# Where the last heads of layer 1 are stored, and when their output product runs

## The chip, the cores and the metric

The kernel runs on one core of a Trainium2 chip. Its five engines work at the same time and are tied together by semaphores: TensorE (PE in the profile, with its weight loads as PEld), VectorE (DVE), ScalarE (ACT), GpSimd (POOL), and SyncE (SP), which here issues the DMA transfers. The metric is the device time of one execution, in microseconds; lower is better. Times are given as the median of several runs.

## The reference

Four attention layers are applied one after the other to `x`, of shape 4 batches x 1024 rows x 256 features, with 16 heads of 16 features each and a context of 77 rows per batch. All arithmetic is in 32-bit floats.

- Layer 0: layer norm, causal self-attention over the 1024 rows and the 77 context rows, then two norms and a feed-forward block of width 1024.
- Layer 1: two attentions side by side. A linear one over the context (`lin`) and a sliding-window one over the last 64 rows (`win`):

```
linear_out = (linear_out / (normalizer + EPS_DEN)).reshape(B, T_dec, D_MODEL)
window_out = jnp.einsum('bhts,bshd->bthd', probs, v_win).reshape(B, T_dec, D_MODEL)
combined = jnp.concatenate([linear_out, window_out], axis=-1)
return residual + combined @ Wout
```

- Layer 2: cross-attention to the context. The scores are multiplied by a given weight per entry and masked, then softmax, values, output product, residual and layer norm.
- Layer 3: cross-attention to the context with heads of 64 features, RMS norm before it, residual after it.

The change concerns the end of layer 1 (`combined @ Wout` for the last half of the heads of the last batch) and the start of layer 2.

## The kernel before, in words

`x` stays on the chip for the whole kernel, one tile per batch (`xs[b]`, 8 row blocks of 128 rows x 256 features). A manual schedule is in force (L94): each engine executes its instructions in the order in which the Python code emits them.

*Memory.* `wpool` holds weights; each of its tags is one slot that successive weights share. Tag `s1`, 2048 floats per partition, first holds layer 0's query and key weights and from unit (3,3) of layer 0 on layer 1's (`w1q`, L1010, made by `plain_pair`, L116). `work` holds the working tiles of layers 0 and 1; the tag `lw` in it has four slots of 1024 floats per partition. After layer 1 `work` is closed (`first.close()`, L1663), and the pool `late`, with the working tiles of layers 2 and 3, takes its place in memory (L1664), so that a tile of `late` can only be written when the tiles of `work` have had their last readers. `small` lives through the kernel; its tag `sT` has two slots. In PSUM, `sm` has three slots in rotation for all small products and transposes, `big` two for scores, and `pv` one.

*Layer 1.* A unit is a batch and a `quad` of four heads; there are 16 units, and the loop at L1650 to L1654 runs each unit's maxima beside the exponentials and products of the unit before. `weights1` (L1179) makes the tiles `lin` and `win` for each pair of quads, that is for half of the heads, and returns the six items that fill them. An item's result goes through `settle` (L533): ACT copies the product from PSUM, PE transposes it, DVE divides and writes it to `lin` or `win` (L551).

`combine1(b, half)` (L1246) adds the output product of one half to `x`. It is a generator of 12 steps: for each of four pairs of row blocks, four PE transposes of `lin` and `win` into `ptc` (L1254), an ACT copy to `cT` (L1256) and a step end; another step end; four products of two matmuls' depth each, eight matmul records in the profile, into `po1` (shown as `po`), a DVE addition to `x` (L1267) and a step end. For all halves but the last it runs as a job beside the units (L1609 to L1613). The last one, `combine1(3, 1)`, runs alone at L1662, after everything pending has been flushed (L1661) and before `work` is closed.

*Jobs.* A `Job` (L436) has a generator, its number of steps `n`, and a start and an end share `a` and `b`: at share s of the stage it has done n x (s - a) / (b - a) steps, rounded up. With `rest` true what is left is done at the end of the stage.

*Start of layer 2.* In this order (L1664 to L1669): `late` is opened, SP loads the keys `kb`, the first weight and mask tile (`side`) and the folded values U of batch 0; then `prep2(0)` turns `x[0]` by 16 PE transposes (`ptx`, L338) with DVE copies (L342) and makes the queries by 16 matmul records (`pp`) with ACT evictions (L1334).

*Layer 2's tiles.* `slot2` (L1350) handles one block of 128 rows. For tile i it issues: the loads of the next side tile; a POOL clearing of the new score tile `s` (L1290); for tile i-1 the 16 exponentials on ACT (L1366); for tile i the score products `ps` in two halves, each multiplied by the weights on DVE (L1378), and the masking (L1383); the first gap for jobs; the value product `po2` of tile i-4 on PE; the maximum `nm` (L1395, L1399); the transposes `psT` of tile i-3 with ACT copies to `pT` (L1285, L1286); the second gap for jobs; the row sums of tile i-1 (L1411, L1412) and their division on POOL (L1413). `slots` (L1671) runs eight tiles per batch and offers the gaps of tile k at shares (k + 0.4)/8 and (k + 1)/8. `jobs2` (L1695) names the jobs of a batch: for batch 0 the load of U and the preparation (`prep2`) of batch 1. Layer 3 (`slot3`) follows in the same manner.

## Time and profile before

| | us |
|---|---|
| median of 3 runs | 2475.52 (2474.48 to 2475.53) |
| the profiled execution | 2472.59 |
| its span, first to last instruction | 2470.9 |
| busy in the span: PE, DVE, ACT, POOL | 2284.0, 1398.5, 1033.3, 640.5 |

The profiled execution is one run, and its own time is what its rows add up to; the runs' median is some 3 us above it. Busy times are averages over stages with different limits. A timeline row gives the start, the busy time, the engine, the source line and operation, what is written from what, and in brackets the idle time before it and what ended it. Helpers have one line for all that pass through them: nearly all matmuls carry L45. The weight loads (PEld) overlap the matmuls. The granted clock is the share of full speed that TensorE's clock had, 1.00 being full.

By the trace layer 1's last window product (`pvw`) starts at 1848.83, the last combine runs from 1850.95 to 1866.9, and the first score product of layer 2 starts at 1875.24.

### The profile page before, as it was taken

The numbers are of one execution on the slowest core, as the hardware profiler recorded it, in microseconds if no ns is written. First come the engines' busy times: TensorE is split into PE (matmuls) and PEld (weight loads), VectorE is DVE, ScalarE is ACT, GpSimd is POOL, SyncE is SP. The second block draws the span as 40 slices with busy tenths as digits, with TensorE's granted clock in tenths as the row PEclk, the third lists the DMA queues.
The fourth block names the chain that finished last, engine by engine and source line by source line (L and its number), as shares of the span: only waits on it lengthen the run. The fifth ranks groups of instructions, "written<-read, shape, count | busy, mean of one in ns | idle before, by whom it ended". The sixth has DMA issues, their size and how long they took to land.

```text
span 2470.9 us, 39772 instructions
## 1 busy us (share of the span) xinstructions
PE 2284.0 (92%) x16162; PEld 1376.6 (56%) x16162; DVE 1398.5 (57%) x2347; ACT 1033.3 (42%) x1716; POOL 640.5 (26%) x923
## 2 busy tenths in 40 slices
PE   5789989898998989989999999999997999899999
PEld 3433434344444544445456766666654777788887
DVE  4446456654466444665436345454436899776664
ACT  1244344344344334433453343444444677532222
POOL 2011013111131111311134223333341366643222
PEclk9699999999999999999999999999998999999999
DMA  6402021100000000010000100111104334022200
GB/s 176 115 25 93 6 72 41 45 6 14 1 6 15 6 14 2 5 35 5 14 6 14 19 16 15 19 19 19 19 1 151 124 120 133 28 52 57 54 14 18
DMA packets 87136, 98.49 MB, mean 40 GB/s; under 512 B 31222, under 2 KB 77866, under 8 KB 86826
## 3 DMA queue, kind: packets, MB, share of 16 engines
q1 hardware_dynamic: 86954, 95.95, 14.5%
q8 instruction: 128, 2.10, 0.4%
q14 instruction: 54, 0.44, 0.1%
HBM read 57.70 MB, written 20.59 MB: 32 GB/s over the span
## 4 chain that ended last, share of the span: by engine, by line
PE 78%; DVE 11%; ACT 6%; issue 2%; POOL 1%; DMA 1%; SPq 1%; ACTq 0%; DVEq 0%; POOLq 0%
PE ps L45 33%; PE po L45 15%; PE pp L45 6%; PE pv L45 5%; DVE mpart L601 5%; PE ph L45 4%; PE ppv L45 2%; PE psT L1285 2%; PE pvw L45 2%; ACT pe L666 2%; PE ptx L338 1%; PE pvl L45 1%; PE pk L45 1%; PE pt L542 1%; PE pm L525 1%
## 5 line engine op out<-in xcount | busy, mean ns | idle before, releaser
L45 PE MATMUL ps<-qk 32*128 32x192 f32 (+8 forms) x5760 | 616.5, 468 | 102.1 <-DVE mpart L601 54.4
L666 ACT ACTIVATE pe<-ps 128x1024 f32<-128x1024 f32 (+2 forms) x384 | 363.2, 952 | 612.2 <-PE ps L45 607.0
L601 DVE TENSOR_REDUCE mpart<-ps 128x2 f32<-128x1024 f32 (+3 forms) x448 | 409.0, 933 | 349.1 <-PE ps L45 348.7
L45 PEld LDWEIGHTS ps<-qk 32*128 32x128 f32 (+1 forms) x5760 | 288.2, 185 | 375.0 <-DVE mpart L601 134.1
L45 PE MATMUL po<-U,pT 128*128 128x256 f32 (+1 forms) x1280 | 290.5, 382 | 7.4 <-DVE x L1405 4.7
L45 PEld LDWEIGHTS po<-U,pT 128*128 128x128 f32 (+1 forms) x1280 | 239.8, 191 | 50.0 <-ACT pT L1286 8.0
L669 POOL TENSOR_SCALAR_AFFINE_SELECT pe<-pe 128x256 f32<-128x256 f32 (+1 forms) x192 | 95.0, 495 | 637.0 <-ACT pe L666 636.1
L1056 DVE TENSOR_REDUCE mrow<-ps 128x4 f32<-128x768 f32 x128 | 122.5, 957 | 141.4 <-PE ps L45 141.0
L1286 ACT COPY pT<-psT 128x512 f32<-128x512 f32 (+1 forms) x192 | 92.0, 517 | 228.1 <-PE psT L1285 228.0
L1131 ACT ACTIVATE pew<-ps 128x768 f32<-128x768 f32 x128 | 103.4, 811 | 173.4 <-PE ps L45 172.6
L1136 POOL TENSOR_SCALAR_AFFINE_SELECT pew<-pew 128x512 f32<-128x512 f32 x128 | 81.6, 637 | 342.0 <-ACT pew L1131 342.0
L45 PE MATMUL pv<-pe,va 128*32 128x512 f32 (+3 forms) x1536 | 165.0, 518 | 0.1
L45 PE MATMUL ps<-G,xT 128*128 128x308 f32 x512 | 143.0, 423 | 0.0
L45 PE MATMUL ph<-yT,w 128*128 128x256 f32 x512 | 138.1, 405 | 0.8 <-DVE qk L527 0.8
L1366 ACT ACTIVATE s<-s,nm 128x77 f32<-128x77 f32 x512 | 131.2, 352 | 15.9 <-DVE nm L1399 15.9
L1498 POOL TENSOR_TENSOR s<-s,den 128x1232 f32<-128x1232 f32 x32 | 72.0, 2249 | 207.7 <-DVE den L1497 192.4
L45 PEld LDWEIGHTS ph<-yT,w 128*128 128x128 f32 x512 | 93.6, 198 | 52.6 <-issue 39.1
L45 PE MATMUL po<-w,hT 128*128 128x256 f32 x512 | 117.0, 382 | 0.0
L45 PEld LDWEIGHTS ps<-G,xT 128*128 128x128 f32 x512 | 92.4, 190 | 26.8
L45 PEld LDWEIGHTS po<-w,hT 128*128 128x128 f32 x512 | 95.4, 190 | 21.0 <-issue 9.1
L527 DVE TENSOR_TENSOR qk<-pm,qk 128x512 f32<-128x512 f32 x64 | 44.0, 688 | 105.2 <-PE pm L525 105.2
L818 DVE TENSOR_SCALAR hT<-ph,c_L_xattn_b 128x256 f32<-128x256 f32 x128 | 61.3, 480 | 72.4 <-PE ph L45 65.2
(191 smaller groups left out, 3175.7 us busy)
## 6 DMA issues: line engine op xcount, KB each, us to landing
side<-in_fside_t SPq DMA_DIRECT2D x32, 616.0 KB
qk<-st SPq DMA_DIRECT2D x256, 64.0 KB
U<-kept_u SPq DMA_DIRECT2D x8, 1152.0 KB
side<-in_mask_t SPq DMA_DIRECT2D x32, 154.0 KB
G<-kept_g SPq DMA_DIRECT2D x4, 1232.0 KB
x<-in_x SPq DMA_DIRECT2D x8, 512.0 KB
out<-x SPq DMA_DIRECT2D x32, 128.0 KB
kept_u<-st SPq DMA_DIRECT2D x21, 154.0 KB
```

What stands on the lines that cost most here:

```text
L45: nc.tensor.matmul(o, lhsT, rhs, start=start, stop=stop, **kw)
L601: nc.vector.tensor_reduce(mpart[bl][:, i, 2 * p : 2 * p + 2, ci], ps[:, :, o : o + w], axis=AX.X, op=ALU.max,)
L666: nc.scalar.activation(pp[:n, :, o:512], ps[:n, :, o:512], AF.Exp, scale=SC)
L669: nc.gpsimd.affine_select(out=own, in_=own, compare_op=ALU.is_ge, fill=0.0, base=0, pattern=[[0, 2], [0, k], [1, P]], channel_multiplier=-1,)
L818: nc.vector.tensor_scalar(h[:, f, :], ph, cols["L0_xattn_b1"][:, 4 * half + f : 4 * half + f + 1], None, ALU.add,)
L1056: nc.vector.tensor_reduce(mo, ps.rearrange("p j (i n) -> p j i n", i=2)[:, :, :, 0 : P + WIN], axis=AX.X, op=ALU.max, negate=True,)
L1131: nc.scalar.activation(pp[:, :, :, 0 : P + WIN], ps.rearrange("p j (i n) -> p j i n", i=2)[:, :, :, 0 : P + WIN], AF.Exp, scale=SC,)
L1136: nc.gpsimd.affine_select(out=pf[:, :, 0:P], in_=pf[:, :, 0:P], compare_op=ALU.is_ge, fill=0.0, base=0, pattern=[[0, 4], [1, P]], channel_ ...
L1285: nc.tensor.transpose(ps[:, k, :], s[:, P * c : P * c + P], ident)
L1286: nc.scalar.copy(pT[:, 4 * group : 4 * group + n, :], ps[:, 0:n, :])
L1366: nc.scalar.activation(hs, hs, AF.Exp, bias=p1["nm"][:, h : h + 1], scale=SC)
L1498: nc.gpsimd.tensor_tensor(s3, s3, den.unsqueeze(2).to_broadcast([P, H, S]), ALU.mult)
```

## The change

For the last batch, the second half's `lin` and `win` are no longer two tiles of tag `lw` in `work`, but the two halves of one tile of 2048 floats per partition in `wpool`, tag `s1`, the slot that held `w1q`. The call of `combine1(3, 1)` before `work` is closed is gone; the same generator becomes a job of layer 2's batch 0, the first in the list, with 12 steps from share 0 to share 0.45.

```diff
     def weights1(u):
-        if u["quad"] % 2 == 0:
+        if (u["b"], u["quad"]) == (NB - 1, 2):
+
+            w = wpool.tile([P, 2048], F32, name="lw3", tag="s1")
+            w = w.rearrange("p (k t n) -> p k t n", k=2, n=P)
+            shared["lin", NB - 1, 1], shared["win", NB - 1, 1] = w[:, 0], w[:, 1]
+        elif u["quad"] % 2 == 0:
             for key in ("lin", "win"):
                 shared[key, u["b"], u["quad"] // 2] = work.tile(
                     [P, NT, P], F32, name=key, tag="lw", bufs=4
...
     flush()
-    run(combine1(3, 1))
     first.close()
...
     def jobs2(b):
         j = []
+        if b == 0:
+            j.append(Job(combine1(NB - 1, 1), 12, 0.0, 0.45, True))
         if b + 1 < NB:
             j.append(Job(loads2(b + 1), 1, 0.4, 0.41))
             j.append(Job(prep2(b + 1), 12, 0.1, 0.95, True))
```

## The prediction

> **What bounds the kernel now.** I read first the table of windows around the seam between layer 1 and layer 2, since every edit lies there. Columns: window, length, busy time of PE, PE's weight loads, DVE, ACT and POOL, granted clock, DMA share, GB/s.

> ```profile
> 1850.00:1856.00 6.00, 5.01 (x15) 4.08 (x16) 0.68 (x2) 0.79 (x2) 0.00 (x0) 0.50 0.01 3
> 1856.00:1866.00 10.00, 7.81 (x38) 6.08 (x38) 2.08 (x3) 1.76 (x3) 0.21 (x2) 0.97 0.14 37
> 1866.00:1876.00 10.00, 10.00 (x39) 5.21 (x39) 3.08 (x5) 2.71 (x4) 0.00 (x0) 1.00 1.01 369
> 1876.00:1888.00 12.00, 5.86 (x38) 3.12 (x34) 11.74 (x14) 5.43 (x23) 0.00 (x0) 0.83 0.40 133
> 1888.00:1900.00 12.00, 7.90 (x25) 4.14 (x26) 11.76 (x14) 8.71 (x32) 4.65 (x4) 0.75 0.56 176
> ```

> Three stages with different limits. Until 1866 PE, ACT and DVE take turns and the loads stand still (3 and 37 GB/s). Until 1876 PE is full. From 1876 to 1900 DVE is full (11.74 and 11.76 of 12) while PE has 6.1 and 4.1 us free. Second, the chain of waits in order of time, which says what sets the end:

> ```profile
> 1850.26 1.12 PE pt L542 x4
> 1851.37 0.87 PE ptc L1254 x4
> ...
> 1864.21 1.99 PE po L45 x8
> 1866.20 2.04 PE ptx L338 x16
> 1868.24 7.08 PE pp L45 x16
> 1875.32 0.74 PE ps L45 x4
> 1876.08 0.55 DVE s L1378
> ```

> Everything is on the path. `combine1(3,1)` (ptc, cT, po) holds it from 1851.37 to 1866.20, 14.83 us; then come layer 2's first transposes and query product, and the first scores reach DVE at 1876.08. Further on the chain follows DVE to 1893.6, then 16 exponentials on ACT (4.11 us), and from 1898.33 PE without a gap; the first `po2` product starts at 1903.93. Third, the timeline: what else stands behind the combine.

> ```profile
> 1863.57 0.59 ACT L1256 COPY cT<-ptc 128x512 f32<-128x512 f32 x1 [2.58 <-PE ptc L1254]
> 1863.59 0.21 POOL L1290 MEMSET s<- 128x48 f32 x2 [14.81 <-PE ptc L1254]
> 1863.61 0.34 SPq L1666 DMA_DIRECT2D kb<-kept_k  x1
> ```

> SP's first load of layer 2 and POOL's clearing of `s` both start just after the last `ptc`: the `late` pool takes the place of `work`, which the combine's source tiles still occupy.

> **The change part by part.**

> *New place for lin and win.* The tile takes the slot of `w1q`, 2048 floats for 2048. The last product with `w1q` starts at 1756.3, and settles of unit (3,2) write after 1780, so the wait for the slot has ended over 20 us before. Shapes and addresses' strides of the settle writes stay (0.42 us each). Cost 0; without that margin a settle would be late, and it isn't near.

> *Loads released.* The last reader of `work` becomes the last window product `pvw`, which ends near 1849.6. `kb`, the first side tile, the first U and the clearing of `s` move up by 14 us; the queues of SP and POOL hold nothing else, and the combine issues no DMA. Before, the loads issued from 1863.6 had all landed by 1876.1, 12.5 us later. The first scores need only the first two in the queue: 1232 + 770 KB at the 369 GB/s above, some 5.6 us, so about 1856. [...] Cost 0, at most 1.

> *Prologue moved up.* The 16 `ptx` transposes now follow `pt`, from 1851.37 in place of 1866.20; `x[0]` was final long before. But they meet a slow clock. The windows of 1 us at the seam and at another stall:

> ```profile
> 1852.00:1853.00 1.00, 0.27 (x3) 0.04 (x1) 0.13 (x1) 0.59 (x1) 0.00 (x0) 0.50 0.00 0
> ...
> 2116.00:2117.00 1.00, 0.55 (x3) 0.46 (x4) 1.00 (x3) 0.00 (x0) 0.83 (x3) 0.50 0.14 51
> 2117.00:2118.00 1.00, 1.00 (x4) 0.82 (x4) 1.00 (x1) 0.00 (x0) 1.00 (x1) 0.50 0.00 0
> 2118.00:2119.00 1.00, 1.00 (x4) 0.82 (x3) 0.97 (x4) 0.00 (x0) 0.83 (x3) 0.50 0.00 0
> 2119.00:2120.00 1.00, 1.00 (x5) 0.83 (x5) 0.96 (x2) 0.88 (x3) 0.28 (x2) 0.80 0.00 0
> ```

> At the seam the clock is 0.50 from about 1849.7 (0.87 in the window before 1850) to 1856.6 (0.72 in the window after 1856): 6.8 us. PE was idle within it, 0.27 busy at 1852, waiting for `cT`. At 2116, with PE busy from about half a microsecond after the drop, 0.50 lasts only 3.4 us. [...] A group of four `ptx` takes 2.04/4 = 0.51 at full speed, 0.99 slowed by the ratio 0.87/0.45 of the slow and fast `ptc` groups.
> [...] By the row: transposes to 1855.3, 1.26 us do 0.65 of `pp`, the other 6.43 end at 1863.0, DVE at 1863.8: 12.3 earlier. I take 14.0, because the cause of the long row, the wait for `cT`, has left this stretch.

> *The combine put into tiles 0 to 3.* As a job of 12 steps until share 0.45 its four quarters fall thus: `ptc`/`cT` 0 before tile 0's maximum; `po`/add 0 and `ptc`/`cT` 1 after it; 1 and 2 after tile 1's; 2 and 3 after tile 2's; `po`/add 3 in tile 3 before its maximum. Its work: DVE 4 x 0.69 = 2.76, ACT 4 x 0.59 = 2.36, PE 4 x (0.45 + 1.99) = 9.76. So the bounds of what comes back are 2.4 (DVE alone, four adds of 0.61 net: one start to the next overlaps by 0.08) and 9.76 (all of PE on the path). PE's lies in its 10.2 idle us between 1876 and 1900; ACT's copies find ACT idle before each tile's exponentials. To choose I walked it, counting from DVE's first start:
> - DVE starts its tiles now at 0, 5.34, 12.74, 19.62, 25.92 (1876.08, 1881.42, 1888.82, 1895.70, 1902.00). Three adds lie ahead of tile 3: 19.62 + 1.83 = 21.45. Its multiplications and masking take 3.08, so add 3 runs from 24.5 to 25.2.
> - The small PSUM pool has three slots in rotation. `po` 1, 2, 3 fall in one slot, and the next in it is the second `psT` of tile 3. So `po` 3 waits for add 2 (19.5), ends at 21.5, with the query product behind it at 23.5; then the second `psT` waits for add 3, to 25.2. That is a new wait, on an engine with all of layer 2 queued behind it. It replaces the wait that stands there now, in the list of waits:

> ```profile
> PEld psT L1285 <- ACT qT L1334: 2.7, 1, 2.7
> ```

> - From there PE is in one piece: two `psT` 0.66, `pp` 1.98, `ps` 1.24, `pp` 1.91, so `po2` starts at 25.2 + 5.79 = 31.0. Now it starts at 1903.93 - 1876.08 = 27.85. Given back: 3.1 us.

> A clock that drops in the 3 us in which PE waits for add 2 would slow `po` 3 and the product behind it: 2 to 3 us more there; the first `psT` ends at 23.95, so 1.2 of it are slack and 1 to 2 would come on the path.

> **Sum.** -14.0 + 3.1 = -10.9 us. From 1904 on PE carries the chain and the order of work is unchanged, so the shift passes to the end. The profiled execution took 2472.59 (span 2470.9 and 1.7 around it) and would take 2461.7; the median of the runs is 2475.52, and from that it is **2464.6 us**.

> **Rivals.**
> [...]
> *PE does not hide the combine*: its 9.76 us come back in full, -14.0 + 9.76 = -4.2, so 2471.3. For it: from 1900 PE is full, and its clock in the first tiles is 0.83 and 0.75, at which 2.44 us per quarter becomes 4.9. [...]
> *A wait takes the removed one's place*, ending slower. The place is ACT: if each `cT` stands behind a tile's 16 exponentials, its `po`, and behind that PE's next scores, wait for 4.10 us. [...] The 2.7 us row is that pattern. Each quarter would cost 4.10 + 0.59 + 1.99 + 0.69 = 7.4 us, four 29.5, net +15.5: 2491. It decides above 14.0/4 = 3.5 us per quarter. Against: a `cT` is issued before the exponentials of the same tile, which wait for its maximum, and after those of the tile before, which end (4.1 us) before that maximum (4.7 us into the tile).
> *The change does not do what it says*: were the loads still held, for instance by another tile of `work`, until 1863.6, `kb` and the side tile would be there near 1870 rather than 1876, and about 8 - 3.1 = 5 us would be left: 2470.6. Against: every other reader and writer of `work` ends before 1849.7 or so.

> **How the numbers follow.** Clock back after one window, 0.48; low over both, 0.25; only DVE's 2.4 us given back, 0.06 (-11.6, 2463.9); PE not hidden, 0.10; loads held, 0.05; a new wait on ACT, 0.06. A measurement here tells 0.2% (5 us) from no change. The first three are faster, as are about half of the two near 5 us with run-to-run scatter a little in favour: 0.84 faster, 0.10 same, 0.06 slower. The range reaches up to the PE and loads cases, 2471.5, which leaves out the last; below, 3 us under the forecast for scatter (the runs span 1 us and the profiled one lies 3 below them) and a smaller add-back: 2461.5.

> **What would show it.** Right: `kb` issued near 1850; `ptx` straight after `pt`; DVE's first L1378 near 1862; clock 1.00 from about 1853; `ptc` and L1267 between L1378 groups of tiles 0 to 3; DVE above 95% busy there; `psT` of tile 3 waiting for L1267; the first `po2` 31 us after the first L1378 and layer 3 shifted rigidly. Wrong: first L1378 after 1864 (clock or loads), PE waiting for `cT` (the ACT rival), or over 4 us more between first L1378 and first `po2`.

## The result

The changed kernel took 2463.09 us (median of 5 runs, 2462.29 to 2466.65) against 2474.48 for the kernel before in the same comparison: a ratio of 0.9959 with a 95% interval of 0.9947 to 0.9972, 11.4 us less. Forecast were 2464.6, 10.9 us less than the 2475.52 of the runs on which the forecast was built. Single executions of one kernel scatter by some 20 us, the shorter ones with the higher mean granted clock: 35 further runs of the kernel before reach from 2459.98 us at 0.975 to 2478.15 us at 0.967.

The chain of waits of the kernel after, in order of time (start, length, what). It answers to the chain shown before:

```profile
1851.68 0.76 PE pvw L45 x10
...
1853.11 0.66 PE pt L542 x4
1853.76 0.89 PE ptx L338 x8
...
1855.83 7.08 PE pp L45 x16
1862.90 0.74 PE ps L45 x4
...
1863.67 0.55 DVE s L1383
...
1882.37 4.11 ACT s L1371 x16
1886.47 0.58 ACT qT L1339
...
1887.10 0.67 PE psT L1290 x4
...
1888.43 3.68 PE pp L45 x4
1892.11 1.24 PE ps L45 x8
1893.35 1.92 PE pp L45 x4
1895.26 4.32 PE po L45 x20
```

The end of the same stretch in the kernel before:

```profile
1893.60 4.11 ACT s L1366 x16
...
1898.33 0.44 PE psT L1285 x2
...
1898.80 1.98 PE pp L45 x4
```

The combine is gone from between `pt` and `ptx`; DVE's first L1383 (L1378 before) comes right after the prologue. This execution happened to reach the last window product 2.85 us later than the one before did (1851.68 against 1848.83), so absolute starts mislead. Two distances serve as rulers instead: from the last `pvw` to DVE's first score multiplication (**seam**), and from that to the first `po2` product (**filling**).

| profile | seam | filling |
|---|---|---|
| before | 1876.08 - 1848.83 = 27.25 | 1903.93 - 1876.08 = 27.85 |
| after | 1863.67 - 1851.68 = 11.99 | 1895.26 - 1863.67 = 31.59 |

The seam gave 15.3 us and the filling took 3.7 back: 11.5 net. The spans differ by 8.7 (2470.9 to 2462.2), which is 11.5 less the 2.85 by which this execution was late already; after the filling the shift stays as it is. Of the 15.3, 0.94 (12.93 - 11.99) are a clock drop that this execution did not have at the seam and others did (see "The seam once more").

The table of windows of the kernel after, columns as before:

```profile
1852.00:1856.00 4.00, 3.29 (x31) 2.48 (x24) 2.17 (x5) 0.59 (x1) 0.21 (x2) 1.00 0.63 200
1856.00:1863.00 7.00, 7.00 (x18) 2.90 (x19) 0.91 (x2) 2.12 (x4) 0.00 (x0) 1.00 1.03 371
1863.00:1876.00 13.00, 11.24 (x68) 8.19 (x69) 12.16 (x16) 7.50 (x25) 0.00 (x0) 1.00 0.50 173
1876.00:1888.00 12.00, 8.77 (x44) 5.46 (x42) 11.79 (x15) 8.80 (x32) 4.65 (x4) 1.00 0.52 172
1888.00:1895.00 7.00, 6.58 (x17) 2.68 (x17) 5.92 (x9) 3.50 (x13) 2.33 (x2) 0.76 0.35 122
```

The loads run beside the prologue (371 GB/s). In the first tiles DVE is full as before, and PE, which had 6.1 and 4.1 us free per 12, is busy 11.24 of 13 and 8.77 of 12. The clock is 1.00 through the seam and drops once, after 1888.

### The profile page after: what moved, and what is told of

It reads as the page before. It is cut to its first block, busy times and chain, and to the rows that moved or that the text cites. A ratio compares the mean times of both kernels' runs of the same rounds, so it can differ in the third digit from the quotient of the medians.

```text
span 2462.2 us, 39771 instructions
## 1 busy us (share of the span) xinstructions
PE 2283.3 (93%) x16162; PEld 1376.9 (56%) x16162; DVE 1398.5 (57%) x2347; ACT 1032.5 (42%) x1716; POOL 639.3 (26%) x923
## 4 chain that ended last, share of the span: by engine, by line
PE 78%; DVE 10%; ACT 6%; issue 2%; DMA 1%; POOL 1%; SPq 0%; ACTq 0%; DVEq 0%; POOLq 0%
PE ps L45 33%; PE po L45 15%; PE pp L45 6%; PE pv L45 5%; DVE mpart L601 5%; PE ph L45 4%; PE ppv L45 2%; PE psT L1290 2%; PE pvw L45 2%; ACT pe L666 2%; PE ptx L338 1%; PE pvl L45 1%; PE pk L45 1%; PE pt L542 1%; PE pm L525 1%
## 5 line engine op out<-in xcount | busy, mean ns | idle before, releaser
L45 PE MATMUL ps<-qk 32*128 32x192 f32 (+8 forms) x5760 | 617.8, 470 | 102.3 <-DVE mpart L601 54.5
L45 PEld LDWEIGHTS ps<-qk 32*128 32x128 f32 (+1 forms) x5760 | 289.7, 186 | 374.1 <-DVE mpart L601 134.2
L45 PE MATMUL po<-U,pT 128*128 128x256 f32 (+1 forms) x1280 | 292.0, 384 | 7.3 <-DVE x L1410 3.8
L45 PEld LDWEIGHTS po<-U,pT 128*128 128x128 f32 (+1 forms) x1280 | 241.2, 192 | 50.0 <-ACT pT L1291 7.9
L45 PE MATMUL pv<-pe,va 128*32 128x512 f32 (+3 forms) x1536 | 165.3, 519 | 0.0
L45 PE MATMUL ps<-G,xT 128*128 128x308 f32 x512 | 143.0, 423 | 0.0
L45 PE MATMUL ph<-yT,w 128*128 128x256 f32 x512 | 138.1, 405 | 0.8 <-DVE qk L527 0.8
L45 PEld LDWEIGHTS ph<-yT,w 128*128 128x128 f32 x512 | 93.7, 198 | 52.6 <-issue 39.1
L45 PE MATMUL po<-w,hT 128*128 128x256 f32 x512 | 117.0, 382 | 0.0
L45 PEld LDWEIGHTS ps<-G,xT 128*128 128x128 f32 x512 | 92.6, 190 | 26.7
L45 PEld LDWEIGHTS po<-w,hT 128*128 128x128 f32 x512 | 95.5, 190 | 20.9 <-issue 9.1
L818 DVE TENSOR_SCALAR hT<-ph,c_L_xattn_b 128x256 f32<-128x256 f32 x128 | 61.3, 481 | 72.4 <-PE ph L45 65.3
```

Of the source, the lines that this page charges most:

```text
L45: nc.tensor.matmul(o, lhsT, rhs, start=start, stop=stop, **kw)
L818: nc.vector.tensor_scalar(h[:, f, :], ph, cols["L0_xattn_b1"][:, 4 * half + f : 4 * half + f + 1], None, ALU.add,)
```

## The experiments

Since single executions scatter, I read the two rulers from each profile beside the times. The question after the result was which of the steps had made the 11 us: the combine off the path, the loads released, the clock; and what made the filling longer.

### The seam once more

The kernel after, unchanged.

> The changed kernel once more, for a second profile of the seam. Main theory: 2463 us, within 1; from the last window product (pvw) to DVE's first L1383 12 to 14 us, depending on whether the clock drops there, and from that to the first po2 product 30 us, or 31.5 if the clock drops in tile 3. If the seam of the first profile, with its clock at 1.00 throughout, was an exception, this profile shows 0.50 after pvw again and 1 to 2 us more there.

2461.63 us, ratio 0.9953 to the kernel before (0.9941 to 0.9966). Seam 1858.42 - 1845.49 = 12.93, filling 1889.96 - 1858.42 = 31.54. The windows of 1 us at this seam:

```profile
1846.00:1847.00 1.00, 0.31 (x7) 0.09 (x2) 0.00 (x0) 0.59 (x1) 0.21 (x2) 0.72 0.00 0
1847.00:1848.00 1.00, 1.00 (x5) 1.00 (x6) 0.00 (x0) 0.00 (x0) 0.00 (x0) 0.50 0.85 177
1848.00:1849.00 1.00, 1.00 (x7) 1.00 (x6) 0.68 (x2) 0.00 (x0) 0.00 (x0) 0.50 0.85 335
1849.00:1850.00 1.00, 1.00 (x7) 1.00 (x6) 0.92 (x2) 0.00 (x0) 0.00 (x0) 0.58 1.02 414
```

Here the clock does drop after `pvw`: by these rows it is at 0.50 from 1846.44 to 1849.84, 3.4 us, and PE is busy from `pt` at 1846.91 on, 0.47 us after the drop. The first profile was a seam without a drop. Over all profiles with `ptx` right after `pt`, this one and those below, the seam is either 12.0 (no drop) or 12.9 (0.50 for 3.4 us); none has more. Both profiles with the combine in the seam (before, and the next one) have 0.50 for 6.8 us in a row and 27.3 us. From the last `pvw` to the end of the span those two take 622.1 us each, and the three profiles of the changed kernel 610.5, 611.4 and 610.5.

### Only the new place

```diff
     flush()
+    run(combine1(3, 1))
     first.close()
...
-        if b == 0:
-            j.append(Job(combine1(NB - 1, 1), 12, 0.0, 0.45, True))
```

> Only the new place: lin and win of the last half lie in the weights' slot, but the combine still runs alone before layer 2. So layer 2's first loads are free to start some 14 us earlier and nothing else moves. Main theory (the gain is the combine's 15 us on the path, the loads were hidden anyway): 2474.5, no different from before within 1. Rival (the gain is the loads released earlier): between 2463 and 2468.

2474.1 us, ratio 1.0002 (0.999 to 1.0013): nothing. The windows of this kernel, and the row of its timeline for the first load:

```profile
1850.00:1856.00 6.00, 4.72 (x15) 3.78 (x16) 0.68 (x2) 1.08 (x2) 0.20 (x2) 0.50 0.82 307
1856.00:1866.00 10.00, 7.81 (x38) 6.14 (x37) 2.08 (x3) 1.76 (x3) 0.00 (x0) 0.96 0.67 227
1866.00:1876.00 10.00, 10.00 (x39) 5.22 (x39) 3.08 (x5) 2.40 (x4) 0.00 (x0) 1.00 0.00 0
```

```profile
1850.01 0.34 SPq L1671 DMA_DIRECT2D kb<-kept_k  x1
```

The loads start at 1850.0 instead of 1863.6, and from 1866 to 1876 the DMA engines have nothing left to do (0 GB/s, where the kernel before has 369). Yet DVE starts at 1876.39, 27.26 us after `pvw`. The earlier loads alone are worth nothing. By the order in which the pools are opened and closed they are what the move of the combine needs, since `late` could not be filled while `work` was still read; no run tried the move without them.

### The combine left out

```diff
-        if b == 0:
-            j.append(Job(combine1(NB - 1, 1), 12, 0.0, 0.45, True))
```

> The combine of the last half is left out, so its product is missing from batch 3; all else is as in the changed kernel. What it gains over the changed kernel is what the combine costs there. Main theory: 2.0 us (full clock) to 3.7 (clock drop in tile 3), so about 2460. If the combine were hidden completely: 2463. If PE's whole 9.8 us were on the path: 2453.

2461.25 us, ratio 0.9946 (0.993 to 0.9963). Six runs from 2452 to 2464.6 can't tell 0.4 us from 3.7, so the profile has to. Seam 12.93, filling 1890.86 - 1861.61 = 29.25. That is 2.3 less than the changed kernel's 31.54 with the same kind of seam. Its chain in tile 3 and 4:

```profile
1883.83 0.69 PE psT L1290 x2
1884.52 3.18 PE pp L45 x4
```

The query product takes 3.18 where it took 1.98 in the kernel before: the clock is at 0.50 here too, from 1883.8 to 1887.2, without any combine. So the combine costs about 2.3 us where it now stands, and the slow clock in tile 3 is a cost of its own, which the kernel before did not have at that point: its drop came earlier, at 1884 to 1894, and PE stood still for most of the first half of it (busy for 0.80 of 5.12 us). (This profile has an earlier drop too, at 1873.5 to 1880.4, but DVE starts tile 3 at 19.60 us after its first start, as in the kernel before with 19.62.)

### The combine in later tiles

```diff
-            j.append(Job(combine1(NB - 1, 1), 12, 0.0, 0.45, True))
+            j.append(Job(combine1(NB - 1, 1), 12, 0.5, 1.0, True))
```

> The job's share is 0.5 to 1.0 in place of 0 to 0.45, so that the four quarters run in tiles 4 to 7, where PE is full, and not in the filling of the pipeline. Main theory (hidden by PE's free time in tiles 0 to 3 alone): PE's 4 x 2.44 = 9.8 us come back in full, in place of 2 to 3.7, so 6 to 7.8 more than the changed kernel: 2470. Rival (anywhere beside layer 2's tiles is as good): 2463, within 1.

2468.93 us, ratio 0.9979 (0.9968 to 0.999). The product of the first quarter and the transposes of the second in its chain, all on PE:

```profile
1896.29 1.99 PE po L45 x8
...
1901.23 0.59 PE ptc L1259 x4
1901.82 4.32 PE po L45 x20
```

In tiles 4 to 7 each `po` (x8; the x20 is the value product `po2`) and `ptc` of the combine stands in the chain with its whole length, since PE has no free time there. As this work lies behind the first `po2`, a longer ruler is needed: from DVE's first multiplication to the first transposes of tile 8 it is 61.56 us in the kernel before (1937.64), 65.31 after (1928.98), 62.96 with the combine left out and 70.89 here (1933.51 - 1862.62). Against the kernel before, 9.3 us come back in place of 3.7; the clock is at 0.50 in the same stretch of tiles 1 and 2 in both, from 7.8 to 18.0 us after DVE's first multiplication. What hides the combine is PE's free time in tiles 0 to 3, and not layer 2 in general.

### What stands in the way in tile 3

The prediction had the second `psT` of tile 3 wait for the combine's last addition. The list of waits of the kernel after says otherwise (who waits, for what: total in us, how often, longest):

```profile
PEld psT L1290 <- ACT qT L1339: 1.9, 1, 1.9
...
PE pp L45 <- DVE x L1272: 1.2, 1, 1.2
```

`psT` waits for the eviction `qT`, which stands behind tile 2's 16 exponentials, as before the change; only the query product ahead of it waits for an addition, the third. The second `psT` starts at 1887.10, before the last addition does, at 1888.04. The prediction and the description of the kernel have the three small PSUM slots in rotation; they are not handed out so: the last quarter's product started at 1879.79, while the third addition, which a rotation would have made it wait for, ended at 1882.92. Two edits test which wait counts. One ends the combine sooner, so that all additions are done in tile 2:

```diff
-            j.append(Job(combine1(NB - 1, 1), 12, 0.0, 0.45, True))
+            j.append(Job(combine1(NB - 1, 1), 12, 0.0, 0.3, True))
```

> The job's share ends at 0.3 in place of 0.45: the four quarters end in tile 2, with two more additions on DVE ahead of tile 2's maximum. Theory from the two profiles (the path in tile 3 leads from tile 2's maximum over 16 exponentials and the eviction qT to the transposes psT): those exponentials start 1.2 us later, 19.9 in place of 18.7 us after DVE's first L1383, and the whole is 1.2 us slower than the changed kernel. The step on record (psT waits in the rotation for the last addition, L1272): that addition now lies before tile 3, and it is 1 to 2 us faster.

2464.19 us, ratio 0.9962 (0.9944 to 0.998). Tile 2's exponentials start at 1882.96 - 1863.11 = 19.85 us, as expected; the filling is 31.79. So no gain from the addition being early, and 0.2 us lost rather than 1.2, since two of the ten `psT` matmuls instead of six are left behind the wait. The other gives the last quarter's product a bank outside the three:

```diff
-            po = sm.tile([P, 2, D], F32, name="po1", tag="sm")
+            if (b, half, q) == (NB - 1, 1, 3):
+                po = pvp.tile([P, 2, D], F32, name="po1", tag="pv")
+            else:
+                po = sm.tile([P, 2, D], F32, name="po1", tag="sm")
```

> The product of the last quarter takes the PSUM bank of the value products, idle until tile 4, in place of one of the three small slots. Theory from the profiles (psT waits for qT behind the exponentials): the second psT still starts just after qT; at most 0.9 us less between DVE's first L1383 and the first po2, because the query product in tile 3 need not wait there for a slot. The step on record (psT waits for the addition of the last quarter): that wait would vanish and 1 to 2 us with it.

2460.17 us, ratio 0.9945 (0.9929 to 0.996). The filling is 1891.51 - 1862.48 = 29.03, 2.6 less, of which 0.9 was expected. Its list of waits:

```profile
PEld psT L1293 <- ACT qT L1342: 3.0, 1, 3.0
```

The wait for `qT` is still there. The other 1.7 us are the clock, which in this profile stays at 1.00 in the tiles; its chain has for the query product 1.98 instead of 3.68:

```profile
1886.38 1.98 PE pp L45 x4
```

So the wait on record is refuted as the cause; whether this edit keeps the clock up by itself or did so in this one profile is open.

### Filling what PE has left

```diff
-            j.append(Job(prep2(b + 1), 12, 0.1, 0.95, True))
+            j.append(Job(prep2(b + 1), 12, 0.1 if b else 0.0, 0.95 if b else 0.6, True))
```

> The changed kernel with the preparation of batch 1 taken at shares 0 to 0.6 in place of 0.1 to 0.95, so that its four query products fall in tiles 1 and 2 and not in 3 and 4. If PE's idle time left in tiles 0 to 3 (some 5 us and 1.7 of slow clock) can be filled: 2 to 4 us faster than the changed kernel, about 2459. If the evictions qT, queued on ACT behind 16 exponentials each, hold PE up in every tile: as fast as the changed kernel or up to 4 us slower.

2455.56 us, ratio 0.9924 (0.9902 to 0.9946). The end of the filling in its chain, and the wait in tile 3:

```profile
1881.48 3.70 PE pp L45 x8
1885.18 0.74 PE ps L45 x4
...
1889.10 0.58 DVE x L1272
...
1889.72 0.44 PE psT L1290 x2
```

```profile
PEld psT L1290 <- DVE x L1272: 0.7, 1, 0.7
```

All four query products are done before tile 3's scores, so no `qT` is between the exponentials and `psT`; what PE waits for now is the wait that the prediction had named, and it is short. To tile 8's first transposes it takes 1923.30 - 1863.9 = 59.4 us, 5.9 less than the changed kernel and 2.2 less than the kernel before. Some 1.7 of the 5.9 are the clock, an estimate from the query product's 3.68 against 1.98: in tile 3 it stays at 1.00 here and in the repetition below. A second comparison, beside the changed kernel:

> The changed kernel beside the two that follow, for a comparison on one chip: 2462, and from pvw to tile 8's first transposes (psT) some 77.3 to 78.2 us.

> The changed kernel with batch 1's preparation at shares 0 to 0.6, once more. If its gain was that PE's idle time in tiles 0 to 3 is filled, it is seen again: some 5 us below the changed kernel, 2457. If it was scatter of five runs: 2462.

2464.22 us (0.9941, 0.9919 to 0.9962) for the changed kernel and 2457.27 us (0.9922, 0.9905 to 0.9939) for the early preparation. The intervals of these two overlap. Their medians are 7 us apart (over all comparisons 2461.63, 2463.09 and 2464.22 against 2455.56 and 2457.27), and the ruler says 5.9 (65.3 in all three profiles of the changed kernel, 59.4 in both of this one). The share 0 to 0.95 moves a single query product:

> As the one before, but shares 0 to 0.95, so that only the first query product moves, from tile 3 into the end of tile 2. If that brings its eviction ahead of tile 2's exponentials, tile 3's transposes need not wait for it: 1 to 2 us faster than the changed kernel, about 2460.5. If the product comes after those exponentials have begun: no difference within 1.

2461.64 us, ratio 0.9945 (0.9926 to 0.9965), and 1926.26 - 1862.29 = 63.97 us to tile 8: 1.3 less than the changed kernel by the ruler, which the times can't tell. `psT` still waits for `qT`, 2.9 us. The last edit joins the early preparation and the other bank:

> The early preparation and the value products' bank for the last quarter's product together. In the early kernel's profile tile 3's last transposes wait 0.5 us for the last addition (L1272); with that product in the other bank the wait goes, and PE waits nowhere else there: 0.5 to 1 us below the early kernel, 2456.5. If the next thing (DVE, or the exponentials) takes the wait's place: no difference.

2457.72 us, ratio 0.9932 (0.992 to 0.9944), and 59.2 us to tile 8: the wait for the addition is gone from its list, and no difference can be measured.

## Why the prediction was right

*New place, cost 0, and loads released, cost 0.* Right. `kb` was issued at 1852.57, just after `pvw`, and the first scores found their operands there. The kernel with only the new place shows both at once: 1.0002.

*Prologue moved up, 14.0 us.* Right in mechanism, and small by 0.3 to 1.3: the seam went from 27.25 to 12.93 with a clock drop, 14.3, or to 11.99 without one, 15.3. The first is the fair comparison, since the kernel before has the drop in both profiles of its seam. No run shows the 14.0 itself: it was my estimate, with full clock from about 1853, and the runs showed 14.3 and 15.3 in its place. The choice against the 6.8 us of 0.50 in the seam's row (12.3) went the right way, since of the eleven profiles with this seam five have 0.50 for 3.4 us, with full clock again 4.35 to 4.46 us after the start of the last `pvw` (1853.2 to 1853.3 if counted from 1848.83), and six have no drop at all. That the wait for `cT` had made the seam's row long was not shown. What the sum left out is that the drop may not come: I took the beginning of the slow stretch in the one profile of before as given. Both came in executions of one and the same kernel, so this part of the gain could not be forecast (see the last section).

*The combine in tiles 0 to 3, 3.1 us given back.* The size is near, 3.7 by the ruler, the way there is not. DVE's part was exact: tile 3 was to start 21.45 us after the first tile and started at 1885.07 - 1863.67 = 21.40. The step that failed is the PSUM one, "the second `psT` waits for add 3": slots are not taken in rotation, and the wait for `qT` stayed. So the second `psT` started at 1887.10 - 1863.67 = 23.43 us in place of 25.2, and the rest of the way to `po2` took 8.16 in place of 5.79. That the total came near is luck: two errors of about 2 us cancelled.

By the two chains the 3.7 are made of three parts. Two additions ahead of tile 2's exponentials make these start 1.2 later (18.70 us after DVE's first start against 1893.60 - 1876.08 = 17.52). PE's order behind the wait, six `psT` matmuls and a copy in place of two, takes 0.9. The query product at half clock takes 1.7 (3.68 against 1.98). The kernel with the other bank has neither of the last two, and its 29.03 is 1.2 above the 27.85 of the kernel before. That a clock drop near this place would cost 1 to 2 us stood beside the sum and was not in it; it came in all three profiles of the changed kernel (0.50 for 3.4 us in each), one query product later than thought.

*The sum.* -14.0 + 3.1 = -10.9 was forecast; the two profiles gave -15.3 + 3.7 = -11.5, the second of the changed kernel -14.3 + 3.7 = -10.6, the medians -11.4.

*The rivals.* A clock that stays at 0.50 for 6.8 us, as in the seam's row ("low over both" in the chances, 0.25), did not occur at the seam without the combine there. PE not hiding the combine was excluded by the filling, and the kernel with the combine in later tiles shows what it would have been. The wait on ACT did show, in small: the last `cT` was ready to be copied at 1877.6 and waited behind tile 1's exponentials to 1878.89; its product's weight load waited 0.4 us for it, and PE not at all. The price needed to turn the sign, 3.5 us per quarter, was never near.

## What to carry to other kernels

A serial piece at a seam is worth moving if the stage behind it starts with another engine as the bound. Here the free time of the piece's engine was in the filling of the pipeline, before the steady state, and the same piece a few tiles later cost nearly its full price (9.3 of 9.8 us). Look then for what else from the full tiles fits into the filling; here moving the next batch's products forward gained half as much again. A buffer change that frees loads can be worth nothing alone and still be what makes the move possible.

## What the runs showed of the hardware

In the kernel after the clock dropped in tile 3, to 0.50 at 1888.5 (the row from 1888 has a mean of 0.75), with PE busy for 1.29 of the 3.41 us before that:

```profile
1885.00:1886.00 1.00, 0.40 (x4) 0.16 (x2) 1.00 (x3) 1.00 (x5) 0.70 (x1) 1.00 1.06 349
1886.00:1887.00 1.00, 0.00 (x0) 0.00 (x0) 0.96 (x2) 1.00 (x4) 1.00 (x1) 1.00 0.99 335
1887.00:1888.00 1.00, 0.90 (x6) 0.62 (x6) 1.00 (x1) 0.72 (x3) 0.63 (x2) 1.00 0.94 313
1888.00:1889.00 1.00, 0.57 (x2) 0.46 (x2) 1.00 (x3) 0.65 (x2) 0.00 (x0) 0.75 0.17 50
```

In the kernel before, PE was busy for 1.64 of the 3.41 us ahead of the drop at 1849.7. I had looked for drops where PE stands still, and had put the one in tile 3 beside the sum.

At the seam the drop lasted 3.4 us in the five profiles in which PE was busy from 0.36 to 0.47 us after it until the clock was back, and 6.8 us in the two profiles in which PE stood still for 0.73 us inside (the wait for the combine's `cT`). The wait was not tried alone, so that it is the reason is not shown.
